# A four-layer scan and attention network on one core: the slot for other stages' TensorE and VectorE pieces moves from behind a round's first scan to behind its third

## The chip, the core and the metric

The kernel runs on one core of a Trainium2 chip. The metric is the device time of one execution in microseconds (us). All numbers are from that one core.

## The reference, cut to what matters

The input is x[4, 56, 56, 96] in float32: four images of 3136 places with 96 channels. Four layers follow each other. Layers 0 and 1 hold a selective scan, layers 2 and 3 a linear attention and a quantized feed-forward part.

```python
# layers 0 and 1: u is the projected input with 192 channels; 4 directions, 16 states
dt = softplus(dt_raw @ dtw + bias)
h[t] = exp(dt[t] * A) * h[t-1] + dt[t] * B[t] * u[t]     # for each channel and state
y[t] = sum over states of h[t] * C[t]
# the directions' y are summed, + u * D; in layer 0 then gate, projection and a GELU
# feed-forward; layer 1 has two 3x3 convolutions, a normalization and a fusion
# layers 2 and 3, on tokens t
t = t + attention(norm(t))      # without softmax: q (k^T v)
t = t + W2 @ relu(W1 @ quantized(norm(t)))
```

The scan is the large part: 2 layers x 4 images x 4 directions x 192 channels x 16 states x 3136 steps.

## The kernel before, in words

**Rounds.** `scans` (from L623) cuts the scans into chunks of 448 steps (`CS`). A chunk has 8 rounds: two halves e of 96 channels, and in each of them four quarters q of 4 states. A round covers 96 channels x 4 states; these lie as 3 groups g (32 channels x 4 states = 128 partitions) beside each other. 2 layers x 4 images x 4 directions x 7 chunks x 8 rounds are 1792 rounds.

**One round n** does, in the order in which it is written:

- `products` (L719, VectorE): h = du * b for groups 0 and 1, where b is the row of B spread over the partitions by a matmul (L616, TensorE, one PSUM bank). Group 2 was made by GpSimd (L714).
- `prepare` (L555): the DMA issues on SyncE (SP) for chunks ahead: the copies of dt, du and of the rows of B and C (`cb`), and GpSimd's `times_u` (L521). dt, du and cb are asked for about three rounds ahead of use.
- the slot "F" (L745), in which other stages place pieces of ScalarE work.
- `prepare_on_scalar` (L581): ScalarE's share in coming chunks (softplus, copies of projected rows).
- `keep_busy` (L778): zero matmuls (L786) that keep TensorE at work, `begin(n + 1)` (L708): the next round's b on TensorE and its group 2 on GpSimd, `add_up` (L788): TensorE sums y over states (L799) for the round before the last, `ahead`: projections for coming chunks (L448, L496, L609).
- three scans (`scan`, L721, one instruction L726 for each group, VectorE). Behind each of them ScalarE's `decay` (L678) makes exp(dt * A) for the same group of the next round into the PSUM bank `da` of this group; there is one bank a group, so a decay waits for the scan that reads the bank. Between the first scan and the second is the slot "C" (L757, L758). At the third, `keep_sums` (L806) copies a finished y out, and `kept` (L696) saves the last state.
- `carried(n + 2)` (L691): ScalarE puts the saved state into the h buffer of the round after the next.
- hc = h * C on GpSimd (L768), which waits for the third scan.

**Other stages.** The rest of the network (`load`, `middle`, `branch`, `fuse`, `attend`) is written as generators. Each of their pieces ends in a `yield` such as "C1 p1.3": the next piece wants a slot C, holds one of two shared PSUM banks (`ps`), and costs TensorE 1.3. "F0 a3.2" wants a slot F and costs ScalarE 3.2. `overlap` (L963) keeps some parts of a stage alive and runs, at each slot, the pieces that want this kind of slot and for which `room` (L1001) finds the backlog small enough; `half_round` lowers the backlog twice a round. So a piece of kind C holds TensorE and VectorE instructions (some GpSimd and SP ones too), and one of kind F holds ScalarE instructions. A typical C piece is a VectorE instruction that reads a matmul's result from the slot before, with a matmul of its own behind it: L1060 (x + ps) and then `factor` (L824); L889 (a normalization's product) and then L1063 or the transposes L1316; L1185 and then L1187; L1192 and then L852; L1203 and L1241 and then L824; L1251 and then L1266. L1310, in the C piece of `gram`, is one on ScalarE. L1083 and L1312 are stores from such pieces. L863 spreads a normalization's factor.

**Order.** The four computing engines follow the order in which the program writes their instructions (`tc.manual_schedule` in `tile_net`); each takes its own instructions one after the other, and waits for those of others where data or a buffer demands it. SP's queue is ordered by the framework. After the last round the remaining pieces run alone (`late`, `alone`).

Of the kernel before, what the change touches and what calls it, by code (L numbers as in the profile page):

```python
# [22 lines left out]
C = 96  # L23
# [144 lines left out]
class Net:  # L168
# [454 lines left out]
    def scans(self):  # L623

        nc, sp = self.nc, self.sp
        chunks = []
        for l in range(2):
            for i in range(NB):
                for n, (orient, rev) in enumerate(ORDER[l]):
                    for step in range(NCS):
                        ch = Step()
                        ch.l, ch.i, ch.orient, ch.rev, ch.step = l, i, orient, rev, step
                        ch.k = 2 * orient + rev if l == 0 else orient + 2 * rev
                        ch.c = NCS - 1 - step if rev else step  # L640
                        ch.n, ch.first = n, n == 0 and step == 0
                        ch.skip = n == 0
                        ch.opening = ch.skip and (l, i) == (0, 0)
                        ch.last = n == 3 and step == NCS - 1
                        ch.cb, ch.dt, ch.du = [], [], []
                        chunks.append(ch)
        rounds = [(ch, e, q) for ch in chunks for e in range(NE) for q in range(NQ)]
        per = NE * NQ


        da = [self.psum.tile([128, 512], F32, name=f"da{g}")[:, : CS + 4] for g in range(NG)]
        for t in da:
            nc.vector.memset(t, 0.0)

        def steps(n):

            return [(ch, n - per * j) for j, ch in enumerate(chunks[max(0, n // per) : n // per + 3], max(0, n // per))]

        def ahead(n):
            for ch, o in steps(n):  # L660
                self.on_tensor(ch, o)

        for n in range(-14, 0):
            for ch, o in steps(n):
                self.prepare(ch, o)
            if n > -8:
                yield "F", n, 0
            for ch, o in steps(n):
                self.prepare_on_scalar(ch, o)
            ahead(n)  # L670
            if n > -8:
                yield "C", n, 0

        def decay(n, g):

            if n < len(rounds):
                ch, e, q = rounds[n]
                nc.scalar.activation(da[g][:, INNER], ch.dt[e][:, g], AF.Exp, scale=ch.par.na[:, e, q, g : g + 1])  # L678

        def column(t, at):  # L680

            return t[:, at : at + 2 * ROW + 1 : ROW]

        def carried(n):

            if n < len(rounds):
                ch, e, q = rounds[n]
                hs[n] = sp.tile([128, WIDE], F32, name="h", bufs=3)
                if not ch.step:
                    return  # L690
                nc.scalar.copy(column(hs[n], ROW if ch.rev else 1), ch.par.carry[:, e, q])  # L691

        def kept(n):
            ch, e, q = rounds[n]
            if ch.step < NCS - 1:
                nc.scalar.copy(ch.par.carry[:, e, q], column(hs[n], 2 if ch.rev else CS + 1))  # L696

        def own(n):
            ch, e, q = rounds[n]
            return NQ * e + q in (OWN_TAIL if ch.l and ch.i else OWN)  # L700

        hs, bs = {}, {}

        def tokens(t):

            return self.groups(t, 2)[:, :, :CS]

        def begin(n):  # L708

            if n < len(rounds):  # L710
                ch, e, q = rounds[n]
                bs[n] = self.spread_b(ch, q)
                if not own(n):
                    nc.gpsimd.tensor_tensor(tokens(hs[n])[:, 2], ch.du[e][:, 2], ch.cb[q][:, 1], ALU.mult)  # L714

        def products(n):
            ch, e, q = rounds[n]
            for g in range(3 if own(n) else 2):
                nc.vector.tensor_tensor(tokens(hs[n])[:, g], ch.du[e][:, g], bs[n], ALU.mult)  # L719

        def scan(n, g):  # L721
            ch, e, q = rounds[n]
            c = 1 if ch.step else 0
            way = slice(CS + 1 + c, 1, -1) if ch.rev else slice(2 - c, CS + 2)
            h = hs[n][:, g * ROW :]
            nc.vector.tensor_tensor_scan(h[:, way], da[g][:, way], h[:, way], 0.0, ALU.mult, ALU.add)  # L726

        carried(0)
        carried(1)
        begin(0)  # L730
        self.exp_and_ln()
        self.tables = True
        for g in range(NG):
            decay(0, g)
        late = []
        for n, (ch, e, q) in enumerate(rounds):
            r = NQ * e + q
            products(n)
            for c, o in steps(n):
                self.prepare(c, o)  # L740
            self.half_round()
            strided = [1.5 + 1.5 * ch.orient] * (r % NQ == 2)
            strided += [1.5 + 1.5 * c.orient for c, o in steps(n) for _ in self.projected(c, o)]
            self.spend((0.6, 0.7, 1.7, 0, 0, 0, 0.7, 0.6)[r], (1.3, 1.3, 0, 0, 0, 0, 0.4, 0.4)[r] + sum(strided))
            yield "F", n, r  # L745
            for c, o in steps(n):
                self.prepare_on_scalar(c, o)
            ended = late.pop(0) if len(late) == 2 else None
            if ended:
                self.keep_busy(ended[2])  # L750
            begin(n + 1)
            if ended:
                self.add_up(*ended)
            ahead(n)
            self.half_round()
            for g in range(NG):
                if g == 1:  # L757
                    yield "C", n, r  # L758
                if g == 2 and ended and ended[2] == NQ - 1:
                    self.spend(0.6, 0)  # L760
                    self.keep_sums(*ended[:3])
                scan(n, g)
                if g == 2:
                    kept(n)
                decay(n + 1, g)
            carried(n + 2)
            hc = sp.tile([128, NG, CS], F32, name="hc", bufs=3)
            nc.gpsimd.tensor_tensor(  # L768
                hc, tokens(hs[n]), ch.cb[q][:, 0].unsqueeze(1).to_broadcast([128, NG, CS]), ALU.mult,
            )  # L770
            late.append((ch, e, q, hc))
            del hs[n], bs[n]
        for ended in late:
            self.add_up(*ended)
        self.keep_sums(ch, e, q)
        yield "C", len(rounds), 0
# [655 lines left out]
```

## Time and profile before

| what | value |
|---|---|
| median of three runs | 8020.21 us (8017.12 to 8021.32) |
| the profiled execution, own time | 8016.8 us |
| its span, first to last instruction | 8014.9 us |
| VectorE busy | 7522.8 us, 94% |
| of it the scans, L726 | 5510.3 us, 5376 of 1073 ns |
| of it the products, L719 | 2019.9 us, 3584 of 605 ns |
| GpSimd busy | 7170.8 us, 89% |
| of it hc, L768 | 4887.1 us, 1792 of 2727 ns |
| TensorE busy, matmuls | 7013.7 us, 88% |
| of it zero matmuls, L786 | 1433.0 us |
| ScalarE busy | 6114.5 us, 76% |
| of it the decays, L678 | 3353.7 us, 5376 of 632 ns |
| granted TensorE clock, mean | 0.907 |

The profile names the engines PE (TensorE), DVE (VectorE), ACT (ScalarE), POOL (GpSimd) and SP (the queue for DMAs); PEld is a weight load. "x" is a count, and a line "A <- B: 28.8, 18, 3.5" in the view of the waits reads: A stood idle until B had ended, 28.8 us in total, 18 times, at most 3.5 us. A line of the timeline has the start in us, the duration in us, engine, line of the kernel, operation, what is written and read, and in brackets how long the engine had stood idle before it and until what. Neighbours of one line are merged there (x2, x8). Durations of successive instructions of VectorE overlap by some 0.05 to 0.1 us, so that busy times of groups add up to a little more than the engine's own.

### The profile page before, as it was taken

The numbers are of one execution on the slowest core, as the hardware profiler recorded it, in microseconds if no ns is written. First come the engines' busy times: TensorE is split into PE (matmuls) and PEld (weight loads), VectorE is DVE, ScalarE is ACT, GpSimd is POOL, SyncE is SP. The second block draws the span as 40 slices with busy tenths as digits, with TensorE's granted clock in tenths as the row PEclk, the third lists the DMA queues.
The fourth block names the chain that finished last, engine by engine and source line by source line (L and its number), as shares of the span: only waits on it lengthen the run. The fifth ranks groups of instructions, "written<-read, shape, count | busy, mean of one in ns | idle before, by whom it ended". The sixth has DMA issues, their size and how long they took to land.

```text
span 8014.9 us, 113446 instructions
## 1 busy us (share of the span) xinstructions
PE 7013.7 (88%) x33765; PEld 2326.8 (29%) x33765; DVE 7522.8 (94%) x9600; ACT 6114.5 (76%) x12759; POOL 7170.8 (89%) x3989
## 2 busy tenths in 40 slices
PE   7888888889888988899889988988889888898888
PEld 3222222222222222222222223322233222332224
DVE  6999999999999999999999999999999999999992
ACT  6778878777778768887678876787877877678776
POOL 5999999999999999999989998999989999899990
PEclk8889989989899989999889999988999999998998
DMA  5556655557555665566655666555565555655552
GB/s 180 181 188 191 197 186 187 173 188 228 186 182 180 222 199 186 170 196 203 196 182 172 195 212 202 180 163 167 185 203 170 167 172 191 192 172 169 174 171 70
DMA packets 568239, 1467.53 MB, mean 183 GB/s; under 512 B 108034, under 2 KB 337156, under 8 KB 566756
## 3 DMA queue, kind: packets, MB, share of 16 engines
q1 hardware_dynamic: 566848, 1458.49, 57.0%
q8 instruction: 265, 4.34, 0.2%
q14 instruction: 354, 2.90, 0.1%
q10 hardware_dynamic: 772, 1.80, 0.1%
HBM read 1186.49 MB, written 273.47 MB: 182 GB/s over the span
## 4 chain that ended last, share of the span: by engine, by line
DVE 32%; PE 31%; ACT 17%; issue 13%; POOL 4%; DMA 2%; DVEq 0%; SPq 0%; POOLq 0%; ACTq 0%
DVE h L726 23%; DVE h L719 7%; PE y L799 6%; ACT da L678 5%; PE y L786 5%; PE y L795 4%; PE b L616 3%; POOL hc L768 2%; PE pp L496 2%; ACT L830 2%; PE ps L947 2%; PE pp L448 1%; ACT Y L806 1%; PE ps L863 1%; PE ps L824 1%
## 5 line engine op out<-in xcount | busy, mean ns | idle before, releaser
L726 DVE TENSOR_TENSOR_SCAN h<-da,h 128x449 f32<-128x449 f32 (+1 forms) x5376 | 5510.3, 1073 | 98.4 <-ACT da L678 82.6
L768 POOL TENSOR_TENSOR hc<-h,cb 128x1344 f32<-128x1344 f32 x1792 | 4887.1, 2727 | 539.7 <-DVE h L726 431.4
L678 ACT ACTIVATE da<-dt,na 128x448 f32<-128x448 f32 x5376 | 3353.7, 632 | 1077.1 <-DVE h L726 1053.3
L719 DVE TENSOR_TENSOR h<-du,b 128x448 f32<-128x448 f32 x3584 | 2019.9, 605 | 96.5 <-PE b L616 62.2
L799 PE MATMUL y<-hc,four 128*32 128x448 f32 x14336 | 1916.1, 610 | 16.0 <-POOL hc L768 15.9
L714 POOL TENSOR_TENSOR h<-du,cb 128x448 f32<-128x448 f32 x1792 | 1756.1, 980 | 46.0 <-ACT h L691 26.3
L786 PE MATMUL y<-w,zeros 128*96 128x448 bf16 x5143 | 1433.0, 397 | 0.0
L616 PE MATMUL b<-cf,sel 128*128 128x448 bf16 x1792 | 672.4, 375 | 731.7 <-DVE h L719 726.7
L786 PEld LDWEIGHTS <-zeros 128*96 128x96 bf16 x5143 | 635.6, 134 | 1177.4 <-issue 1017.9
L448 PE MATMUL pp<-U,wd 96*128 96x448 f32 x896 | 662.6, 828 | 10.9 <-DMA U<-u 5.6
L799 PEld LDWEIGHTS y<-hc,four 128*32 128x32 f32 x14336 | 294.5, 113 | 1232.2 <-issue 719.3
L795 PE MATMUL y<-Y,ident 96*96 96x448 f32 x672 | 537.5, 889 | 35.7 <-ACT Y L806 20.2
L496 PE MATMUL pp<-cf,wd 12*96 12x448 f32 (+1 forms) x896 | 477.9, 615 | 98.3 <-ACT dtc L506 51.9
L521 POOL TENSOR_TENSOR duc<-dtc,U 96x896 f32<-96x896 f32 x224 | 483.3, 2157 | 27.0 <-ACT dtc L508 27.0
L696 ACT COPY carry<-h 128x3 f32<-128x3 f32 x1536 | 302.0, 197 | 263.4 <-DVE h L726 257.6
L806 ACT COPY Y<-y 96x448 f32<-96x448 f32 x448 | 341.7, 763 | 28.2 <-PE y L799 27.2
L691 ACT COPY h<-carry 128x3 f32<-128x3 f32 x1536 | 280.0, 182 | 48.2 <-POOL hc L768 44.9
L587 ACT COPY cf<-pp 64x448 f32<-64x448 f32 x448 | 235.8, 526 | 87.6 <-PE pp L609 79.3
L506 ACT ACTIVATE dtc<-pp,wd 96x448 f32<-96x448 f32 x448 | 281.8, 629 | 17.6 <-PE pp L496 13.3
L616 PEld LDWEIGHTS <-sel 128*128 128x128 bf16 x1792 | 179.0, 100 | 367.3 <-issue 296.7
L496 PEld LDWEIGHTS pp<-cf,wd 12*96 12x96 f32 (+1 forms) x896 | 113.6, 165 | 468.5 <-ACT dtc L506 175.6
L863 PEld LDWEIGHTS ps<-rsb,ident 128*96 128x96 f32 x1768 | 207.3, 178 | 126.3 <-issue 77.6
(383 smaller groups left out, 5392.7 us busy)
## 6 DMA issues: line engine op xcount, KB each, us to landing
cb<-cd SPq DMA_DIRECT2D x896, 448.0 KB, 4.8
dt<-dd SPq DMA_DIRECT2D x448, 672.0 KB, 5.8
du<-dd SPq DMA_DIRECT2D x448, 672.0 KB, 5.5
dd<-dtc SPq DMA_DIRECT2D x672, 112.0 KB, 2.0
dd<-duc SPq DMA_DIRECT2D x672, 112.0 KB, 2.0
win<-m SPq DMA_DIRECT2D x252, 112.0 KB, 4.3
U<-u SPq DMA_DIRECT2D x112, 168.0 KB, 4.8
w<-z SPq DMA_DIRECT2D x84, 224.0 KB, 4.1
```

The lines of the kernel that those rows point to most:

```text
L448: self.nc.tensor.matmul(ch.ps.rearrange("p (a b) -> p a b", b=HS), ch.par.wx[:, e], self.in_order(self.U[e], ch.orient, ch.c * CS, CS), st ...
L496: self.nc.tensor.matmul(ch.pd, ch.par.wt[rows, C * e : C * e + C], ch.cf[rows], start=True, stop=True)
L521: self.nc.gpsimd.tensor_tensor(in_rows(ch.duc), in_rows(ch.dtc), u[:, :, lo : lo + CS // HS], ALU.mult)
L616: self.nc.tensor.matmul(ps, self.sel[:, q], self.upper(ch.cf), start=True, stop=True)
L678: nc.scalar.activation(da[g][:, INNER], ch.dt[e][:, g], AF.Exp, scale=ch.par.na[:, e, q, g : g + 1])
L714: nc.gpsimd.tensor_tensor(tokens(hs[n])[:, 2], ch.du[e][:, 2], ch.cb[q][:, 1], ALU.mult)
L719: nc.vector.tensor_tensor(tokens(hs[n])[:, g], ch.du[e][:, g], bs[n], ALU.mult)
L726: nc.vector.tensor_tensor_scan(h[:, way], da[g][:, way], h[:, way], 0.0, ALU.mult, ALU.add)
L768: nc.gpsimd.tensor_tensor(hc, tokens(hs[n]), ch.cb[q][:, 0].unsqueeze(1).to_broadcast([128, NG, CS]), ALU.mult,)
L786: self.nc.tensor.matmul(self.y[:C], self.zeros[:, :C], self.some, start=False, stop=False)
L795: nc.tensor.matmul(o, w, self.in_order(a, ch.orient, ch.c * CS, CS), start=True, stop=False)
L799: nc.tensor.matmul(self.y[32 * n : 32 * n + 32], self.four, hc[:, g], start=n == 3, stop=n == 3 or q == NQ - 1,)
```

## The change

The slot "C" of a round is offered behind the loop over the three groups, instead of in its second turn. It still stands before `carried(n + 2)` and before hc. So the VectorE instructions of the pieces come behind the third scan, its `kept` and the next round's decays. What is in the pieces, how many of them a slot takes and the slot "F" are not touched.

```diff
             ahead(n)
             self.half_round()
             for g in range(NG):
-                if g == 1:
-                    yield "C", n, r
                 if g == 2 and ended and ended[2] == NQ - 1:
                     self.spend(0.6, 0)
                     self.keep_sums(*ended[:3])
...
                 if g == 2:
                     kept(n)
                 decay(n + 1, g)
+            yield "C", n, r
             carried(n + 2)
             hc = sp.tile([128, NG, CS], F32, name="hc", bufs=3)
             nc.gpsimd.tensor_tensor(
```

## The prediction

> **What bounds the kernel now.** I read the page's busy table first, then the waits of VectorE and TensorE between 130 and 7790 us (the stretch in which scans run, without the fill at the start and the last 225 us), then the timeline at the largest waits.
>
> ```profile
> PE 7013.7 (88%) x33765; PEld 2326.8 (29%) x33765; DVE 7522.8 (94%) x9600; ACT 6114.5 (76%) x12759; POOL 7170.8 (89%) x3989
> PEclk8889989989899989999889999988999999998998
> ```
>
> VectorE is the fullest engine. In the windows view it is busy 7384.6 of those 7660 us, so 275 us are all that a new order of its queue could ever save there. Its waits say where most of the 275 lie:
>
> ```profile
> DVE h L726 <- ACT da L678: 80.0, 173, 1.9
> DVE h L719 <- PE b L616: 52.6, 71, 2.8
> DVE w L889 <- PE ps L863: 28.8, 18, 3.5
> DVE w L1060 <- PE ps L1058: 14.2, 8, 3.3
> DVE h L726 <- POOL h L714: 14.0, 15, 2.0
> DVE w L1203 <- PE ps L1201: 9.9, 9, 2.2
> ```
>
> Columns: total us, times, longest. The lines other than L719 and L726 are the pieces of other stages. All of them in this view add up: 28.8 + 14.2 + 9.9 (shown) + 8.2 + 8.1 + 7.9 + 5.6 + 5.2 + 1.8 + 1.3 + 0.9 = 91.9 us. The VectorE timeline has 85 such waits among 434 pieces, and in it they sum to 92.6.
>
> TensorE, in the same stretch, mostly waits for VectorE's products:
>
> ```profile
> PE b L616 <- DVE h L719: 713.1, 773, 2.7
> ```
>
> So in 773 of 1792 rounds TensorE is early: it stands at the next b until the products have read the one b bank. In the others it is late, by up to some 3 us. A late round looks like this:
>
> ```profile
> 2039.99 1.70 PE L863 MATMUL ps<-rsb,ident 128*96 128x112 f32 x8
> ...
> 2041.48 0.58 PE L616 MATMUL b<-cf,sel 128*128 128x448 bf16 x1
> ...
> 2041.72 0.62 DVE L889 TENSOR_TENSOR w<-w,ps 96x448 f32<-96x448 f32 x1 [3.47 <-PE ps L863]
> ...
> 2042.26 2.07 DVE L726 TENSOR_TENSOR_SCAN h<-da,h 128x449 f32<-128x449 f32 x2
> ...
> 2044.25 1.12 DVE L719 TENSOR_TENSOR h<-du,b 128x448 f32<-128x448 f32 x2
> ```
>
> The piece L889 stands between the first scan and the other two. It waits 3.47 us for L863, and two scans that need nothing of it, 2.07 us long, stand behind it.
>
> **What the Trainium skill says.** "PSUM — Partial Sum Buffer", Engine vs sequencer instructions: VectorE's and ScalarE's queues are strict first in, first out, and matmuls start in program order. The trace agrees: the two scans above start only after L889. "Perfetto Trace Analysis", Optimization Strategy: look for the gaps on the most contended engine within the stretch concerned, and for what ends them; that is the table above. "TensorE: Matmul & The Clock Gate", What's actually happening: a TensorE idle for a window of about 3.4 us falls to half clock. The eight L863 here took 1.70 us, and 1.01 in a busier round at 5315.86; the mean granted clock is 0.907.
>
> **The change, part by part.** The order of the instructions (of both programs, as built) shows: TensorE's order is the same up to the last 4% of its queue, since the scans issue nothing on it. ScalarE's differs by L1310 alone (56 times 0.57 us), which now stands behind the round's last decays. GpSimd's differs at the very end only. On VectorE all 434 pieces move from behind the first scan to behind the third. None is removed: their 0.6 us each stay.
>
> (1) *Saved on VectorE.* A piece is reached two scans later, 2.07 us by the row above; I use 2.14 (twice 1.07), an upper value. Of the 92.6 us of waits, 10 are longer than 2.14 and keep 7.2, so 85.4 can go. But a VectorE that arrives earlier also needs the next b earlier. In the timelines I took, for each of the 85 waits, the least time by which b (L616) ended ahead of its products (L719), over the rounds from there until TensorE was early again. In 27 places it is less than the saving. At 2041.72, for instance, the b of the round after the next ends at 2047.64 and its products start at 2048.26, 0.62 us later: of 2.14 only 0.62 remain. These take back 16.1. Saved: 85.4 - 16.1 = 69.3 us: 2 us up to 1000, 31 from 1000 to 5000, 36 after.
>
> (2) *Added on TensorE.* Where a piece has a matmul after its VectorE instruction, TensorE now waits until the third scan and the piece have ended. An example from the timelines: L1060 starts at 2050.40, its L824 at 2052.34. Moved, L1060 ends about 2053.1, L824 begins at 2053.3 and ends 0.92 later; with the 0.56 us of zeros behind it, b begins at 2054.8 instead of 2054.10. That is some 0.65 late, and it has about 2.4 us until its products. The same sum for all rounds with a piece (median TensorE work behind it 1.66 us; 1.2 us of this fit beside the two products that delay b anyway) gives 259 rounds in which b comes later, by 170 us together. Against the time that b has to spare there (median 2.4 us per round), 18 places exceed it, by 6.5 us. Cost: 7 us. Behind b in TensorE's queue stand y (L799) and the projections; their readers are a round or more away.
>
> (3) *Added on ScalarE.* A piece's matmul feeds ScalarE in the next round (squares, Silu, Gelu), ahead of that round's decays. After the third scan ScalarE has a carry copy, a decay and a carry, 0.20 + 0.63 + 0.18 us; the matmul is then there about 0.62 + 0.92 + 0.3 us after that scan: a new wait of up to 0.9 us. The next decay can start only when a further scan has ended (0.62 + 1.12 + 1.07 us), and its own scan is 3 us beyond that. ScalarE waits 1053 us for such scans today, which hides it. Not shown by the trace is how often it meets a heavy round. From below it is a gain: where a piece stands behind the third scan, ScalarE has 0.6 us more up to the next first scan, which could take a quarter off the 80.0 us of da waits (-20). From above: 0.9 us in one of six of the 259 rounds, +40. I take +10.
>
> (4) *Moved DMAs and GpSimd work.* SP's stores of these pieces (L1083, L1312) wait some 2 us longer, with loads of cb, dt and du queued behind them. Those are issued about three rounds (13 us) ahead and land in 4.8 to 5.8 us; VectorE waits for du 7.2 us in all. At nothing; without that cover, 2 us for each of 84 stores would be 168. GpSimd's pieces (L1053, L1214) keep their place between L714 and L768: nothing. VectorE's leftover after the last scan is 121 instructions before and 122 after: nothing, give or take 5 us.
>
> Sum: -69 + 7 + 10 = -52 us. The profiled execution took 8016.8 us (its span 8014.9), 3.4 below the median of 8020.2; I take the difference off the median: 8020 - 52 = **7968 us**. Steps 2 to 4 with their bounds give 7938 to 7998.
>
> **The rivals.**
> *A larger gain (10%).* TensorE is no obstacle and ScalarE's extra room counts: -69 + 7 - 20 = -82, 7938 us. For it: 1754 ScalarE waits for scans show that it is mostly early. Against: the da waits come behind Gelu and Silu with their table loads, 3 us long.
> *The wait moves to b (15%).* From 1000 to 5000 us TensorE is itself the limit: a tenth of these rounds have b ready within 0.11 us of need. Then the 31 us there come back at L719, and only 38 - 17 = 21 remain, or less: 8010 us, no change that can be measured.
> *TensorE falls behind (15%), slower.* The 170 us of later b add up instead of being absorbed: a TensorE that stands longer and then works in bursts runs more often at half clock (1.70 instead of 1.01 us for the same eight matmuls), and so doesn't catch up before the next piece. Its place is L719 behind L616. It decides once more than 69 of the 170 us, 41%, reach VectorE; at 60% it is 102 - 69 = +33, 8053 us. Against it: 713 us of TensorE's waiting for products in the same stretch, and the filler matmuls L786 are as many as before.
> That the change doesn't do what it says is excluded by the order of the instructions.
>
> **How the numbers follow.** The forecast has 60%, the rivals 10, 15 and 15. A measurement can tell about 0.2%, 16 us, from no change. Faster: 60 + 10 = 70%; same 15%; slower 15%. The range runs from a little below the larger gain (7925, for the 5 us of leftover and a da wait more) to the upper edge of no change, 8036; it leaves out the slower rival.
>
> **What would show it.** Right: in VectorE's waits the eleven piece lines fall from 92 to some 10 to 25 us; L719 waiting for L616 goes from 53 to about 75 (16 and 7 more); L726 waiting for da stays within 60 to 120; TensorE's wait for products (713) shrinks, and new TensorE waits for pieces appear, some 150 us. VectorE's busy time stays at 7520. Wrong: b waits over 120 us, or a granted clock below 0.89, would mean that TensorE has become the bound; da waits over 150 would put the fault on ScalarE.

## The result, and the profile after

The changed kernel took 7954.44 us in the median of 4 runs (7941.06 to 7956.18), against 8018.66 us of the kernel before beside it: a ratio of 0.9922, 95% interval 0.9910 to 0.9934. Its profiled execution, 7941.06 us with a span of 7939.3, is the fastest of the four. In a later job on one chip with other kernels the same program took 7937.38 us (4 runs, ratio 0.9904, 0.9891 to 0.9918). The forecast was 7968 us, a gain of 52; measured are 64 and 81.

The lines of the code behind the change are numbered one lower from here on (L888 is L889 of before, and so on); up to L756 they are the same. In the kernels of the experiments they can stand one or two higher.

The page of the changed kernel, busy times and granted clock:

```profile
PE 6970.5 (88%) x33762; PEld 2314.2 (29%) x33762; DVE 7516.4 (95%) x9603; ACT 6104.3 (77%) x12756; POOL 7165.1 (90%) x3989
PEclk8989989989999989989889899999999898998988
```

Nothing was taken from VectorE's work: 7516.4 us busy, as against 7522.8. The time went out of its waits. The view of VectorE's waits in the stretch of the scans (130 to 7715 us; total, times, longest):

```profile
DVE h L726 <- ACT da L678: 73.5, 156, 1.9
DVE h L719 <- PE b L616: 67.4, 86, 4.5
DVE h L726 <- POOL h L714: 14.2, 13, 2.0
...
DVE w L888 <- PE ps L862: 5.8, 4, 2.5
DVE w L1059 <- PE ps L1057: 3.7, 4, 1.5
```

The waits of the other stages' pieces fell from 91.9 to 10.4 us: the two lines at the end and one of 0.9. The products' wait for b rose from 52.6 to 67.4, the scans' wait for da fell from 80.0 to 73.5. All waits of VectorE up to the last scan sum to 193.3 instead of 271.4 us, 78.1 less. That scan starts at 7724.3 instead of 7809.3 us, 85.0 earlier. The other 7 us come from VectorE's busy time in this stretch, 7397.1 instead of 7404.9 (idle gaps too short for the view grew by some 0.8 us). Why VectorE is busy for 7.8 us less stays open. Behind the last scan 9.5 us come back: the leftover takes 214.0 us, before 204.5.

What TensorE does in exchange, in its waits in the same stretch:

```profile
PE b L616 <- DVE h L719: 589.5, 628, 2.7
...
PE ps L1315 <- DVE xra L888: 27.1, 23, 2.2
```

It now stands at the pieces (all such lines together 100 us; before, 0.3) and stands 124 us less at b (713.1 before). The same place as in the timeline shown for the kernel before, the piece L889 behind a late L863:

```profile
2020.06 3.05 DVE L726 TENSOR_TENSOR_SCAN h<-da,h 128x449 f32<-128x449 f32 x3
...
2022.32 0.93 PE L862 MATMUL ps<-rsb,ident 128*96 128x112 f32 x8
...
2023.08 0.36 PE L616 MATMUL b<-cf,sel 128*128 128x448 bf16 x1
...
2023.29 0.62 DVE L888 TENSOR_TENSOR w<-w,ps 96x448 f32<-96x448 f32 x1 [0.17 <-PE ps L862]
...
2023.82 1.14 DVE L719 TENSOR_TENSOR h<-du,b 128x448 f32<-128x448 f32 x2
```

The three scans are one merged line now, no piece between them. L862 still ends late, at 2023.25, but the scans run meanwhile, and L888 waits 0.17 instead of 3.47 us. Not all of that is the move: TensorE had its full clock here (granted share 1.00 from 2021.5 to 2023.3 us; 0.50 in the round shown before), and the eight matmuls took 0.93 instead of 1.70 us. Between the first scan and the second, L888 would have waited about 2.1 us in this execution (an estimate: from the first scan's end at about 2021.1 to 2023.25). b was ready at 2023.44, in time for the products at 2023.82.

### The profile page after: what moved, and what is told of

Read it like the earlier page. It is cut to its first block, busy times and chain, and to the rows that moved or that the text cites. A ratio compares the mean times of both kernels' runs of the same rounds, so it can differ in the third digit from the quotient of the medians.

```text
span 7939.3 us, 113478 instructions
## 1 busy us (share of the span) xinstructions
PE 6970.5 (88%) x33762; PEld 2314.2 (29%) x33762; DVE 7516.4 (95%) x9603; ACT 6104.3 (77%) x12756; POOL 7165.1 (90%) x3989
## 4 chain that ended last, share of the span: by engine, by line
DVE 30%; PE 29%; ACT 19%; issue 14%; POOL 4%; DMA 3%; DVEq 0%; SPq 0%; POOLq 0%; ACTq 0%
DVE h L726 22%; DVE h L719 6%; ACT da L678 6%; PE y L798 6%; PE y L785 5%; PE y L794 3%; POOL hc L767 2%; PE b L616 2%; ACT L829 2%; PE ps L946 2%; ACT Y L805 1%; PE pp L496 1%; PE pp L448 1%; PE ps L823 1%; POOL h L714 1%
## 5 line engine op out<-in xcount | busy, mean ns | idle before, releaser
L726 DVE TENSOR_TENSOR_SCAN h<-da,h 128x449 f32<-128x449 f32 (+1 forms) x5376 | 5469.0, 1070 | 92.7 <-ACT da L678 76.1
L678 ACT ACTIVATE da<-dt,na 128x448 f32<-128x448 f32 x5376 | 3342.9, 632 | 890.7 <-DVE h L726 875.7
L719 DVE TENSOR_TENSOR h<-du,b 128x448 f32<-128x448 f32 x3584 | 2023.4, 605 | 107.0 <-PE b L616 76.9
L798 PE MATMUL y<-hc,four 128*32 128x448 f32 x14336 | 1894.4, 603 | 12.3 <-POOL hc L767 12.0
L616 PE MATMUL b<-cf,sel 128*128 128x448 bf16 x1792 | 671.5, 375 | 605.1 <-DVE h L719 596.1
L616 PEld LDWEIGHTS <-sel 128*128 128x128 bf16 x1792 | 178.5, 100 | 373.1 <-issue 302.5
L823 PE MATMUL ps<-w,cen 96*96 96x448 f32 x458 | 232.7, 600 | 34.4 <-DVE w L1240 11.7
L496 PEld LDWEIGHTS pp<-cf,wd 12*96 12x96 f32 (+1 forms) x896 | 111.4, 162 | 452.9 <-ACT dtc L506 167.2
```

Of the source, the lines that this page charges most:

```text
L496: self.nc.tensor.matmul(ch.pd, ch.par.wt[rows, C * e : C * e + C], ch.cf[rows], start=True, stop=True)
L616: self.nc.tensor.matmul(ps, self.sel[:, q], self.upper(ch.cf), start=True, stop=True)
L798: nc.tensor.matmul(self.y[32 * n : 32 * n + 32], self.four, hc[:, g], start=n == 3, stop=n == 3 or q == NQ - 1,)
```

## The experiments

Waits below are VectorE's in each kernel's own stretch from 130 us to its last scan. "Pieces" are its waits in the slot's instructions, "b" those of L719 for L616, "da" those of L726 for L678.

### The slot at other places

Three kernels put the same slot elsewhere. One scan later than before, between the second and third:

```diff
             for g in range(NG):
-                if g == 1:
+                if g == 2:
                     yield "C", n, r
```

> The slot lies between the second and the third scan. Theory (the pieces' waits for TensorE and ScalarE are covered by the scans that no longer stand behind them): in the trace of the kernel before, the 85 waits cut at one scan of 1.07 us sum to 65.7 of 92.6 us, against 85.4 at two scans, so three quarters of the change's gain of 64 us: about -49, 7970 us; the piece waits of VectorE sum to about 30 us. Rival (what counts is that the scans, and with them the decays and hc, are no longer put off by the pieces' 0.6 us of work, whatever they wait): half the scans behind a piece are freed, half the gain: about -32, 7987 us.

One scan earlier, ahead of the first:

```diff
-                if g == 1:
+                if g == 0:
                     yield "C", n, r
```

> The slot lies between the products and the first scan, one scan earlier than in the kernel before. Theory: each of the 85 waits grows by about 1.07 us, 91 us, some pieces that had less than a scan to spare wait anew, and part is given back at b: 8080 to 8130 us, piece waits 150 to 230 us. Rival of the pieces' work alone: one more scan behind each piece, +32, about 8050 us, and the piece waits hardly change.

Later than in the change, behind the next round's products:

```diff
             products(n)
+            if n: yield "C", n - 1, (r - 1) % per
             for c, o in steps(n):
...
-                if g == 1:
-                    yield "C", n, r
```

> The slot's VectorE pieces lie behind the next round's products, ahead of that round's first scan: 1.1 us later than in the change, and at the same place of VectorE's queue as with the slot before the first scan, but a round later. Theory: the 10 us of piece waits left go to about 2; but TensorE's matmul behind a piece no longer fits beside the products, so b comes later in 550 us instead of 170 us of sum, and some 46 instead of 7 us of that reach VectorE: 20 to 40 us slower than the change, 7975 to 7995 us, with waits of L719 for b at 90 to 120 us. Rival (the place of the pieces' work among the scans): as with the slot before the first scan, slower than before, 8050 us.

And, run in a later job to look between the last two, between the two products of the next round:

```diff
-        def products(n):
+        def products(n, gs):
             ch, e, q = rounds[n]
-            for g in range(3 if own(n) else 2):
+            for g in gs:
...
-            products(n)
+            products(n, (0,))
+            if n: yield "C", n - 1, (r - 1) % per
+            products(n, (1,))
...
-                if g == 1:
-                    yield "C", n, r
```

> The slot's VectorE pieces lie between the two products of the next round, half a microsecond later than in the change and half earlier than behind both products (8045 us, where b and da waits were 60 and 49 us above the change's). Theory (the give-back grows with how late TensorE's and ScalarE's share of a piece comes, b and da both, and sets in above what fits beside the two products): half to a third of these 109 us, b waits 85 to 100 and da waits 85 to 100 us, 7985 to 8010 us. Rival (the loss behind both products belongs to the pieces standing right ahead of the first scan, where they put off a scan that has its da already): about as the change, 7950 to 7965 us.

Each ratio is to the kernel before as it ran in the same job (8018.66 us beside the change, 8019.79 beside the first three kernels of this section, 8020.11 beside the fourth). The waits are those of one profiled execution each.

| slot | median us | ratio to before, 95% | pieces | b | da |
|---|---|---|---|---|---|
| ahead of the first scan | 8223.62 | 1.0259 (1.0246 to 1.0273) | 298.7 | 63.9 | 60.2 |
| behind the first scan (before) | 8018.66 | 1 | 91.9 | 52.6 | 80.0 |
| behind the second | 7965.42 | 0.9934 (0.9923 to 0.9946) | 34.3 | 62.2 | 70.9 |
| behind the third (the change) | 7954.44 | 0.9922 (0.9910 to 0.9934) | 10.4 | 67.4 | 73.5 |
| between the next round's products | 8008.22 | 0.9984 (0.9975 to 0.9993) | 0.9 | 99.9 | 104.4 |
| behind the next round's products | 8045.41 | 1.0036 (1.0023 to 1.0049) | 0.0 | 127.7 | 122.8 |

The pieces' waits fall with every step back, 299, 92, 34, 10, 1, 0 us, and up to the third scan the time follows them. The intervals of the second and the third scan just touch; the change's second measurement (0.9904, 0.9891 to 0.9918) lies apart from the second scan's. Behind the second scan the theory expected about 7970 us and 30 us of waits, and the rival, for which the pieces' work counts and not their waits, 7987; measured are 7965 and 34.3, and 7987 lies outside the interval. Ahead of the first scan the direction was right, but the size was far off: 204 us slower instead of 60 to 110. The waits of the pieces rose by as much as the time (298.7 - 91.9 = 206.8 us; all other kinds together fell by 10, and busy time rose by 10). It was their number that was underestimated: 256 pieces wait there instead of 84. VectorE's waits show it: L1082, which waited 9 times before, now waits in all its 28 parts. L889 waits 32 times (18 before), L1203 18 times (9):

```profile
DVE w L889 <- PE ps L863: 44.1, 32, 3.5
DVE w L1082 <- PE ps L1080: 36.1, 28, 2.2
DVE w L1203 <- PE ps L1201: 31.3, 18, 4.3
```

The granted clock was lower as well, 0.891 instead of 0.907; how much of the pieces' longer waits is due to that isn't separated.

Behind the next round's products the expectation failed: 20 to 40 us slower than the change were expected, 91 were measured. The rival of the place among the scans is out as well: VectorE's queue has the pieces at the same place as in the slowest kernel, and it is 178 us faster. Two waits take the gain back:

```profile
DVE h L719 <- PE b L616: 127.7, 139, 2.8
DVE h L726 <- ACT da L678: 122.8, 198, 3.6
```

The b wait rose by 60 us over the change, where 46 - 7 = 39 had been worked out. The da wait rose by 49, and that had been left out altogether. ScalarE's waits point to the reason for da. First the change, then the kernel with the slot behind the next products:

```profile
ACT da L678 <- DVE h L726: 867.3, 1647, 4.4
...
ACT w L837 <- PE ps L823: 124.9, 108, 5.1
```

```profile
ACT da L678 <- DVE h L726: 775.6, 1501, 2.7
ACT w L839 <- PE ps L825: 247.8, 143, 5.6
```

The squares (L837, L839) wait for the matmul of a piece, 124.9 us in the change and 247.8 here, and behind them in ScalarE's queue stand the decays of the next round. The traces bear this out: of the 49 us, 36 lie in rounds in which ScalarE waited for a piece's matmul, or had done so in the round before (30.3 us of da waits there in the change, 66.8 here). The half-way kernel tests it. Its time and b fell within what was expected, near the upper ends (8008 us of 7985 to 8010, 99.9 of 85 to 100); da, 104.4, is 4 above its range. Its profiled execution, 7990 us, is the fastest of eleven, so that its waits are those of a faster execution than the median. The rival, about as fast as the change, is out. So both kinds of waits rise together as soon as the slot passes the third scan.

### The slot moved in a part of the rounds

```diff
             for g in range(NG):
-                if g == 1:
+                if g == 1 and n >= 1120:
                     yield "C", n, r
...
+            if n < 1120: yield "C", n, r
             carried(n + 2)
```

> The slot is moved in rounds 0 to 1119 only (the first 4900 us); from 1120 on it lies between the first and second scan as before. Theory: these rounds hold 42.5 of the 85.4 us that can go, and 31.8 of the 69.3 that remain after what b takes back: about half of the change's 64 us, 7985 to 7992 us; the piece waits fall in these rounds alone, and the leftover after the last scan takes as long as before, 204 us. Rival that goes by the number of pieces: 149 of 434 are in these rounds, a third: 7997 us.

Measured: 7982.48 us, ratio 0.9957 (0.9945 to 0.9969), 37 us faster than before, and 48.2 us of waits of pieces, 43.7 fewer (42.5 expected). That is about half of the gain (37 of 64 or of 81) with a third of the pieces (149 by the expectation; the trace has 136 of the 434 in these rounds). The rival's 7997 us lies just outside the interval, but it would lie inside if the gain of 81 were divided, so that the time alone doesn't decide. The traces do. In this kernel rounds 0 to 1119 end 29.5 us earlier than before, and rounds 1120 to 1679, where nothing is moved, take only 3.8 us less. In the two profiles of the change the same two stretches gain 40.6 and 46.0, and 33.6 and 36.7 us. So the gain lies where the slot is moved, and nearly half of it in the rounds with a third of the pieces. The leftover behind the last scan took 204.5 us, as before the change.

### The leftover at the end

The same with 1680 in place of 1120, so that only the last 112 rounds keep the old place:

```diff
-                if g == 1:
+                if g == 1 and n >= 1680:
                     yield "C", n, r
...
+            if n < 1680: yield "C", n, r
```

> The slot is moved in rounds 0 to 1679; in the last 112 it lies between the first and second scan as before. With the change, the last scan ended 85 us earlier but the leftover behind it took 214.0 us instead of 204.5; with the slot moved in the first 1120 rounds alone, 204.5. Theory (the leftover is longer because the order at the very end, and so the parts that are still alive there, differs): the leftover takes 204 to 206 us again, and nearly all of the gain stays, 2 or 3 us of waits come back in the last rounds: 7945 to 7950 us, faster than the change by 5 to 9. Rival (the longer leftover belongs to a faster scan stretch or to chance of the granted clock): 212 to 216 us and 7955 us.

Measured: 7947.74 us, ratio 0.9909 (0.9896 to 0.9923), leftover 204.6 us. That met the expectation, but its interval and the change's overlap, so it was run again beside the change on one chip:

> The change itself once more, on one chip with the next two kernels, so that they can be told from it: 7945 to 7958 us, the leftover after the last scan 212 to 216 us. If the leftover is 204 us here, its length is chance and not the order at the end.

> The kernel with the slot moved in rounds 0 to 1679 once more, beside the change: by the theory of the leftover 4 to 9 us faster than the change, leftover 204 to 206 us. If both take the same time within 3 us, the shorter leftover is given back in the last rounds or lost in the spread.

Measured: the change 7937.38 us, ratio 0.9904 (0.9891 to 0.9918), leftover 209.7; the other 7949.20, ratio 0.9919 (0.9907 to 0.9932), leftover 204.5. The leftover is shorter here where the end keeps its order (204.5 to 204.6 in three profiles, 209.7 and 214.0 with the change), but no shorter time comes of it: in the first job this kernel was ahead by 7 us, in the second the change by 12. Executions of the change alone spread from 7931 to 7956 us. The two profiled executions of the change differ by 16 us at the last scan already, spread over all kinds of waits (193.3 and 210.8 us in all). So this kernel isn't shown to beat the change.

But the order at the end alone doesn't explain the longer leftover. The traces of all kernels, with the granted clock of the leftover alone, speak for the rival, the clock:

| kernel | VectorE's order in the leftover | clock there | leftover us |
|---|---|---|---|
| before; slot ahead of the first scan; slot moved in rounds 0 to 1119; in rounds 0 to 1679 (two profiles) | old | 0.86 | 204.4 to 204.6 |
| slot behind the second scan | old | 0.85 | 207.3 |
| slot moved in rounds 0 to 1679, more filler matmuls (below) | old | 0.83 | 211.5 |
| the change | the change's | 0.79 | 214.0 |
| the change once more | the change's | 0.81 | 209.7 |
| the change, fewer filler matmuls (below) | the change's, but for one pair | 0.83 | 203.1 |
| slot between the next round's products; behind them | a third one | 0.87; 0.88 | 198.4; 198.5 |

With one and the same order the leftover takes between 204.4 and 211.5 us, and in the old order as in the change's it is longer where the clock is lower. At a clock of 0.83 the change's order isn't the longer one. TensorE is busy for 176.0 us of the leftover in the change and for 167.2 before, with fewer matmuls (988 and 1023). Why the clock is lower there in the change stays open.

### More and fewer filler matmuls

What remains at b could be lateness of TensorE that the fillers L786 add to, or a lack of clock. The change with fewer of them:

```diff
-WARM, PER_P = 6.8, 1.6
+WARM, PER_P = 5.0, 1.6
```

> The change, with 3325 filler matmuls (L786) instead of 5140, about 1.0 a round less. Theory A (TensorE's lateness behind the moved pieces is what is left at b, and the fillers stand ahead of the next b): L719's waits for b fall from 67 to about 45 us and the da waits by some 5, 7925 to 7940 us. Theory B (the fillers keep the granted clock up, and a slower TensorE is later still): the clock falls from 0.913 to below 0.89, b and da waits rise by 20 to 60 us, 7975 to 8015 us.

Measured: 7967.38 us, ratio 0.9936 (0.9924 to 0.9949), 13 us above the change's first measurement. The two intervals overlap a little, but all five executions (7961 to 7977) are longer than all eight of the change (7931 to 7956). The granted clock fell from 0.913 to 0.874; b rose to 80.0 and da to 93.1 us. That is theory B's side, at a smaller size than it said (7975 to 8015).

```profile
DVE h L726 <- ACT da L678: 93.1, 178, 2.5
DVE h L719 <- PE b L616: 80.0, 70, 4.6
```

Then more of them, with the slot moved in rounds 0 to 1679:

```diff
-WARM, PER_P = 6.8, 1.6
+WARM, PER_P = 8.0, 1.6
```

> The slot moved in rounds 0 to 1679, with 6495 filler matmuls instead of 5143, about 0.75 a round more. With fewer fillers the clock fell from 0.913 to 0.874 and the time rose by 13 us. If the clock is what TensorE lacks behind the moved pieces: clock 0.92 to 0.93, b and da waits 10 us lower, 7930 to 7942 us. If TensorE's time ahead of b is what it lacks: b waits rise from 70 to 85 us or more, 7955 to 7970 us.

Measured: 7947.83 us, ratio 0.9913 (0.9899 to 0.9926), against 7949.20 with the usual number on the same chip: no difference. The clock rose to 0.925, but b to 81.4 us (76.1 with the usual number); da was 72.6 (77.3). Neither expectation holds as a whole: the clock rose as in the first, and the time lies between the two. That a faster clock and a longer queue ahead of b cancel would fit, but isn't shown; the profiled execution, 7966.5 us, is the slowest of five. Neither number of fillers beats the usual one, and neither lowers b.

## Why the prediction was right, point by point

**The bound.** VectorE, with 275 us of waits in the stretch of the scans as all that could be won: right. 78 us of VectorE's waits went.

**Step 1, the saving.** 85.4 us were to go at the pieces; 81.5 went (91.9 to 10.4), in the second profile of the change 78. The slot behind the second scan supports the way it was worked out, by cutting each wait at the time of the scans put ahead: 65.7 expected there, 57.6 measured.

**Steps 1 and 2 at b.** 16.1 taken back and 6.5 of new lateness were to raise b from 53 to about 75. Measured are 67.4 and, in the second profile of the change, 70.8. The forecast of 150 us of TensorE's new waits for pieces was high (100 and 95), and its wait for products shrank by 124 us: the slack was there and was used. That it is used up soon behind the third scan is shown by the two kernels beyond it, not by the prediction, whose accounting gave 39 us for the slot behind the next products where b rose by 60.

**Step 3, ScalarE.** This is the term with the wrong sign: +10 us were forecast, -6.5 and -5.0 measured (da 73.5 and 75.0). Before the change ScalarE's waits from 130 to 7790 us had these two lines (their counterparts after it stand under "The slot at other places"):

```profile
ACT da L678 <- DVE h L726: 1040.3, 1734, 4.0
...
ACT w L838 <- PE ps L824: 29.2, 41, 1.9
```

The new waits for TensorE are there: up to the last scan all of ScalarE's waits for it rose from 320 to 454 us. But its waits for scans at the decays fell from 1047 to 870. The one kind took the place of the other, and on balance the scans waited no longer for their decays. The price exists all the same, one step further: between the next products it is 31 us over the change, behind them 49. Why da fell below 80 at all isn't settled. The gain that the prediction allowed for, 0.6 us more room on ScalarE, can't be the whole of it: with the slot behind the second scan there is no more room, and da is 70.9. A difference of this size also appears where nothing is moved: in rounds 1120 to 1679 da is 22.1 us before, and 18.2 in the kernel that moves the slot in earlier rounds only.

**Step 4, DMAs, GpSimd, the end.** VectorE's waits for du are 2.9 us (7.2 before): nothing, as said. The leftover was set to zero, give or take 5; it was 9.5 and 5.2 us longer. It goes with the clock granted there, and the order alone doesn't explain it, as the table of the leftovers shows.

**The sum** by the terms as measured in the first profile: pieces -81.5, b +14.8, da -6.5, all other waits -4.9, busy time -7.8, leftover +9.5, together -76.4; the spans differ by 75.6. The profiled execution was 13 us faster than its median, so that the medians show 64. In the second profile the pieces give -78.0, b +18.2, da -5.0, all other waits +4.0, busy time -8.1 and the leftover +5.2: -63.7, with spans that differ by 63.5. So the forecast overpriced da by 15 to 16.5 us and b by 4 to 8. In part its total came near by luck: the first profile's busy time, leftover and other waits stood at nothing in the forecast, and their -7.8, +9.5 and -4.9 us nearly cancel.

**The rivals.** That the wait moves to b, or that TensorE falls behind, did not happen at this place. Half a scan further back most of the gain is lost, and behind the next round's products the time is slower than before by 0.2 to 0.5%, with b and da at 128 and 123 us. The larger gain was forecast at 7938 us, and the change's second measurement is 7937; but its cause, 20 us less of da waits, did not come (6.5 and 5.0).

## What to carry to other kernels

On an engine that takes its instructions in order, an instruction that may wait belongs behind the work that doesn't need it, as far as its own consumers allow; the saving could be read here from the trace before by cutting each of its waits at the time of what is put ahead. Then look at who waits for the moved instruction: here two engines had 700 and 1000 us of idle time that took the delay, and half a microsecond further back they no longer did. Of the six places tried, the fastest was the one at which the waits of the moved instructions had nearly gone and the others' had not yet grown. With a gain of 0.8 to 1%, look at the spread of single executions, and at the clock in each stretch, before a further few microseconds are credited to anything.

## What the runs showed of the hardware

**Filler matmuls and the clock.** With 1815 fewer of them TensorE's granted clock went from 0.913 to 0.874 and the kernel's time from 7954 (7937 in the second measurement) to 7967 us. With 1352 more (slot moved in rounds 0 to 1679) the clock went from 0.912 to 0.925, and the time stayed (7949 and 7948).

**When the clock falls.** The prediction quotes the rule that a TensorE idle for a window of about 3.4 us falls to half clock. This trace doesn't show that rule, and the measurement decides. In the trace of the kernel before, the records of the clock know full and half speed only, and all of their stretches but one are multiples of 3.41 us. The late round of the prediction lies in a stretch of 20.48 us at half speed that begins at 2023.51. In the 3.41 us ahead of that fall TensorE had full clock and was busy with matmuls for 2.01 us. Of the 283 falls between 130 and 7700 us, none had 3.41 us without a matmul just ahead of it: the longest pause there was 2.9 us, and the median busy share 60%. The ends of matmuls are modelled in the profile, so these shares are rough.
